# A graph network's dense block: the fused rows are formed in the place of the attention's rows, and the adjacency quarters are asked for one step later

## The chip, the cores and the metric

The kernel runs on one core of a Trainium2 chip. Its time is the device time of one execution in microseconds; the lower the better. The core has five engines[...]: TensorE (PE, matrix products, with its weight loads shown apart as PEld), VectorE (DVE), ScalarE (ACT), GpSimd (POOL) and SyncE (SP, which only issues DMAs). They meet at semaphores. Data lies in SBUF (128 partitions), products land in PSUM, and DMAs move data from and to the chip's main memory.

## The reference

Four graph layers over 4096 nodes of 256 features, with one 4096 x 4096 adjacency of zeros and ones. Each layer normalises its rows, takes the positive part, computes something, and adds it to the rows. The change lies in layer 0, in the part after its attention:

```python
h_enh = silu(_ln(Wh @ fe1_w + fe1_b, fe_ln_g, fe_ln_b)) @ fe2_w + fe2_b
B, C, dt = split(Wh @ W_bcdt + b_bcdt, 3, axis=1)
ab = softmax(dt + A[None, :], axis=1) * B @ abp_w + abp_b
h_part, z = split((Wh * ab) @ W_hz + b_hz, 2, axis=1)
hs = (h_part * silu(z) + h_part * D) @ out_w + out_b
hs = hs * (1.0 + C @ cp_w + cp_b)
comb = concatenate([h_attn, hs], axis=1)
g = sigmoid(silu(_ln(comb @ g1_w + g1_b, g_ln_g, g_ln_b)) @ g2_w + g2_b)
fused = g * h_attn + (1.0 - g) * hs + h_enh
return _ln(fused, ln_g, ln_b)            # and x = x + this
```

`Wh` and `h_attn` come from the attention. Layer 1 divides by the number of ones in each row of the adjacency, so these have to be counted.

## The kernel before

Rows are handled in tiles of 128, four tiles (BT = 4) to a block, eight blocks in all. One large tile `xs` in SBUF holds all 4096 rows. In layer 0 the attention leaves its rows `h_attn` there; at the end of each block's dense part the new rows take their place.

The dense part is the generator `dense(b)`, which yields 30 times. `run_staggered` starts a block every 16 steps and advances all that are active by one step in turn, so that about two blocks are under way: the second half of block b beside the first half of block b + 1. A scheduler then places the instructions of each engine; what the engines run is the order that it makes, not that of the source alone.

In each of a block's first 16 steps `with_counts` also counts a quarter of the adjacency: `ask` has POOL issue a DMA of 128 x 1024 values (L548), and `count` runs two sign activations over it on ScalarE with a running sum (L556). A quarter has one of AHEAD = 4 buffers.

The steps of a block that the prediction speaks of, in order:

- L568: POOL adds `ln_b` to the block's input rows `xt`, which an SP queue has loaded (L565) into the only buffer for them.
- `whT`: TensorE transposes `Wh` in two groups of four (L507); ScalarE copies the first group out of PSUM (L508), VectorE the second (L511). The PSUM pool for transposes has three buffers.
- `bc` (L581), a softmax over part of it (L586 to L596), and `obc` (L598) on POOL.
- `t1` (L607), its normalisation with `fe_off` (L520) on VectorE, and the scaling of it on ScalarE (L523).
- `hidden` turns it and applies silu (L534); `sz` (L631 to L640).
- `henh` (L649): four products and an add of a bias, on VectorE, from PSUM. `hs` (L656): four more. The PSUM pool for products has five buffers.
- `comb` (L663 to L668): `ha`, the block's rows of `xs`, and `hs` are turned in four groups, copied by ScalarE and VectorE in turn. Then POOL takes `dh = ha - hs` (L670) and `hs = hs + henh` (L671).
- `t2` (L677), its normalisation with `gl_off`, `hidden` again, and `f` (L686).
- tanh (L690), L691 and L692 make the fused rows of it; statistics lead to `ol_off`; ScalarE scales (L523); POOL multiplies by `ln_g` (L695) and adds `xt` into `ha` (L696).

In the kernel before, `henh` and `f` carry the same tag in a pool with one buffer per tag, so they take turns in one buffer:

```python
henh = d.tile([P, BT, D], F32, tag="henh", name="henh")   # L645
f = d.tile([P, BT, D], F32, tag="henh", name="f")         # L682
```

Of the kernel before, what the change touches and what calls it, by code (L numbers as in the profile page):

```python
# [11 lines left out]
F32 = mybir.dt.float32  # L12
# [4 lines left out]
ALU = mybir.AluOpType  # L17
# [4 lines left out]
P = 128  # L22
# [6 lines left out]
def run_staggered(gens, period):  # L29

    gens, active, tick = list(gens), [], 0
    while gens or active:
        if gens and tick % period == 0:
            active.append(gens.pop(0))
        for g in list(active):
            if next(g, StopIteration) is StopIteration:
                active.remove(g)
        tick += 1
# [3 lines left out]
def kernel(ctx: ExitStack, tc: tile.TileContext, w: dict, out: bass.AP):  # L42
    nc = tc.nc
    x, adj = w["x"], w["adj"]
    N, D = x.shape
    NT = N // P
    KD = D // P
    BT = 4
# [271 lines left out]
    with ExitStack() as l0:  # L320
# [150 lines left out]
        with ExitStack() as es:  # L471
            d = es.enter_context(tc.tile_pool(name="l0_d", bufs=1))
            AHEAD = 4
# [25 lines left out]
            def wide(t):  # L499

                return t.rearrange("p (o f) -> p o f", o=1).broadcast_to([P, BT, t.shape[1]])
# [26 lines left out]
            def hidden(z, g, b):  # L528

                zT = d.tile([P, KI, BW], F32, tag="zT", name="zT", bufs=2)  # L530
                for k in range(KI):
                    turn(
                        zT[:, k, :], [z[:, i, ts(k, P)] for i in range(BT)],
                        lambda dst, ps: nc.scalar.activation(  # L534
                            dst, ps, AF.Silu, scale=g[:, k : k + 1], bias=b[:, k : k + 1]
                        ),
                    )
                    if k % 2:
                        yield
                return zT  # L540
# [3 lines left out]
            def ask(n):  # L544
                for t, q in asked[len(came) : n]:

                    came.append(code_p.tile([P, QW], BF16, tag="a", name="a", bufs=AHEAD))
                    nc.gpsimd.dma_start(out=came[-1], in_=adj[ts(t, P), ts(q, QW)])  # L548

            def count(g):  # L550

                ask(g + AHEAD)
                t, q = asked[g]
                for v in range(2):
                    sign = code_p.tile([P, QW], BF16, tag="sign", name="sign", bufs=1)
                    nc.scalar.activation(  # L556
                        sign, came[g], AF.Sign, bias=limits[:, v : v + 1],
                        accum_out=over[:, t, v, q : q + 1],
                    )

            def dense(b):
                at = ts(b, BT)
                ha = xs[:, at, :]
                xt = d.tile([P, BT, D], F32, tag="xt", name="xt")
# [80 lines left out]
                henh = d.tile([P, BT, D], F32, tag="henh", name="henh")  # L645
# [33 lines left out]
                yield from normed(t2, "gl")  # L679
                yield  # L680
                g1T = yield from hidden(t2, g_g, g_b)
                f = d.tile([P, BT, D], F32, tag="henh", name="f")  # L682
                for i in range(BT):
                    ps = psm.tile([P, D], F32, tag="mm", name="mm")
                    products(ps, lambda k: g1T[:, k, ts(i, P)], lambda k: g2[:, k, :], KI)
# [7 lines left out]
                yield  # L693
                yield from normed(f, "ol")
                nc.gpsimd.tensor_tensor(f, f, wide(ln_g), ALU.mult)  # L695
                nc.gpsimd.tensor_tensor(ha, f, xt, ALU.add)  # L696

            def with_counts(b):
                at, n = b * BT * NQ, BT * NQ
                for k, _ in enumerate(dense(b)):  # L700
                    if k < n:
                        count(at + k)
                    yield

            ask(AHEAD - 1)
            run_staggered([with_counts(b) for b in range(NB)], 16)


# [360 lines left out]
```

## Time and profile before

| | |
|---|---|
| median of three runs | 3072.19 us (3071.23 to 3072.98) |
| the profiled execution's own time | 3071.94 us |
| its span, first to last instruction | 3070.0 us |
| mean granted TensorE clock over the span | 0.979 |
| PE, PEld, DVE, ACT, POOL busy over the span | 93, 76, 60, 41, 31% |
| dense part of layer 0, from the first quarter counted | 644 to 1256 us |
| of it with counts on ScalarE | 644 to 1126 us |
| one sign over a quarter, and the read of its sum | 1148 ns, 190 ns |
| landing of a quarter's DMA, median | 4.3 us |
| L695 and L696 on POOL | 2348 ns and 2337 ns, medians |

Times count from the span's start. In a line of the timeline the first number is the start, the second the length, then come engine, source line, operation, and written and read tiles; a bracket at the end holds how long the engine had been idle and what ended that. A wait line gives the total, how often, and the longest. An engine that is busy beside others costs nothing unless something waits for it.

### The profile page before, as it was taken

To read this page: it belongs to the slowest core of one execution; us is meant where nothing else is said; L and a number is where in the kernel's file an instruction comes from. 1 tells how busy PE (TensorE), PEld (TensorE's weight loads), DVE (VectorE), ACT (ScalarE), POOL (GpSimd) and SP (SyncE) were. 2 spreads that over 40 slices of the span, in tenths; PEclk is the share of its full clock that TensorE was granted. 3 is DMA by queue.
4 is the path that set the end of the run, shared out by engine and by line. 5 is a ranking of instruction groups with operands and counts; after the bars stand their busy time and mean duration, and the time that the engine had idled before them with its cause. 6 is when DMAs were issued, how large, how long until landed. Compare 5 with 4: busy or idle time off the path is not lost.

```text
span 3070.0 us, 34819 instructions
## 1 busy us (share of the span) xinstructions
PE 2868.8 (93%) x13344; PEld 2341.7 (76%) x13344; DVE 1847.3 (60%) x3298; ACT 1271.1 (41%) x1924; POOL 952.6 (31%) x727
## 2 busy tenths in 40 slices
PE   5799999999999999699968999999999999999999
PEld 4688888866565555588857888788888888888888
DVE  5766766424444444544479888845866666666653
ACT  5555665469999962400044434443211211211211
POOL 3556665534544443100016555561000000000000
PEclk9799999999999999799988999999999999999999
DMA  8566665244544420234222222102111111111100
GB/s 208 130 137 143 127 137 132 66 65 73 79 76 77 75 47 7 88 124 142 91 110 76 89 79 72 71 8 69 59 37 46 49 37 43 52 37 40 53 7 7
DMA packets 105366, 235.18 MB, mean 77 GB/s; under 512 B 10704, under 2 KB 26576, under 8 KB 97008
## 3 DMA queue, kind: packets, MB, share of 16 engines
q0 software_dynamic: 39328, 73.56, 15.6%
q1 hardware_dynamic: 64480, 158.68, 15.0%
q8 instruction: 104, 1.70, 0.2%
q10 hardware_dynamic: 1392, 0.72, 0.1%
q14 instruction: 62, 0.51, 0.1%
HBM read 262.22 MB, written 37.81 MB: 98 GB/s over the span
## 4 chain that ended last, share of the span: by engine, by line
PE 26%; issue 25%; DVE 4%; POOL 2%; DMA 1%; ACT 1%; POOLq 0%; DVEq 0%; ACTq 0%
PE acc L306 11%; PE acc L764 8%; PE s L150 3%; PE mm L150 2%; PE acc L1001 2%; DVE run L229 1%; POOL y L269 1%; DVE y L265 1%; DMA turned<-codesT 1%; POOL out_dram L1014 1%; POOL pl_rs L116 0%; DVE pl_st L121 0%; ACT y L295 0%; ACT h L133 0%; DVE hT L109 0%
## 5 line engine op out<-in xcount | busy, mean ns | idle before, releaser
L306 PE MATMUL acc<-v,y 128*128 128x257 f32 x4096 | 927.7, 385 | 46.1 <-ACT y L295 23.5
L306 PEld LDWEIGHTS acc<-v,y 128*128 128x128 f32 x4096 | 776.3, 192 | 160.5 <-ACT y L295 24.1
L269 POOL TENSOR_TENSOR y<-y,turned 128x1024 f32<-128x1024 f32 x256 | 547.1, 2150 | 313.9 <-DVE y L265 267.1
L295 ACT ACTIVATE y<-y,sdst 128x512 f32<-128x512 f32 x512 | 342.9, 714 | 368.1 <-POOL y L269 367.9
L265 DVE SCALAR_TENSOR_TENSOR y<-ab_row,cdst,b 128x512 f32<-128x512 f32 x512 | 361.7, 742 | 187.9 <-PE acc L306 116.6
L1001 PE MATMUL acc<-v,y 128*128 128x257 f32 x2048 | 454.5, 380 | 0.4 <-DVE rden L1009 0.4
L150 PE MATMUL s<-qT,hT 128*128 128x256 f32 x2048 | 445.2, 380 | 0.7 <-ACT qT L949 0.7
L150 PEld LDWEIGHTS s<-qT,hT 128*128 128x128 f32 x2048 | 389.9, 190 | 53.2 <-ACT qT L949 1.4
L1001 PEld LDWEIGHTS acc<-v,y 128*128 128x128 f32 x2048 | 387.9, 190 | 55.1 <-issue 0.8
L994 ACT ACTIVATE y<-y 128x1024 f32<-128x1024 f32 x128 | 132.2, 1055 | 714.3 <-DVE y L993 710.1
L229 DVE SCALAR_TENSOR_TENSOR run<-turned,sd,run 128x512 f32<-128x512 bf16 x496 | 373.0, 752 | 48.4 <-DMA turned<-codesT 26.8
L1014 POOL DMA_DIRECT2D out_dram<-o x32 | 17.4, 542 | 933.7 <-DVE rden L1009 930.5
L556 ACT ACTIVATE sign<-a,limits 128x1024 bf16<-128x1024 bf16 x256 | 293.9, 1148 | 16.1 <-DMA a<-in_adj_dram 10.4
L764 PE MATMUL acc<-v,eq 128*128 128x512 f32 x1024 | 239.3, 395 | 0.0
L963 DVE SCALAR_TENSOR_TENSOR y<-code,s 128x512 f32<-128x512 bf16 x256 | 175.7, 687 | 100.5 <-PE s L150 100.3
L764 PEld LDWEIGHTS acc<-v,eq 128*128 128x128 f32 x1024 | 192.9, 189 | 44.7 <-DVE eq L760 0.3
L993 DVE TENSOR_TENSOR y<-y,top 128x1024 f32<-128x1024 f32 x128 | 146.2, 1214 | 43.0 <-PE top L987 43.0
L970 DVE TENSOR_TENSOR mx<-mx,y 128x512 f32<-128x512 f32 x224 | 154.9, 691 | 7.4
L362 ACT ACTIVATE turned<-cT,log_wide 128x1024 bf16<-128x1024 bf16 x128 | 141.4, 1105 | 32.1 <-PE cT L357 31.9
L150 PE MATMUL mm<-kept 128*128 128x512 f32 x288 | 135.6, 605 | 9.4 <-ACT kept L508 7.3
L760 DVE TENSOR_SCALAR eq<-code 128x4096 fp32r<-128x4096 bf16 x32 | 73.4, 2292 | 114.9 <-PE acc L764 114.9
L357 PE MATMUL cT<-identb,adj_t 128*128 128x128 bf16 x1024 | 83.2, 226 | 38.1 <-ACT turned L362 19.5
(209 smaller groups left out, 2779.4 us busy)
## 6 DMA issues: line engine op xcount, KB each, us to landing
adj_t<-in_adj_dram POOLq DMA_DIRECT2D x128, 256.0 KB, 4.6
codesT<-turned SPq DMA_DIRECT2D x32, 1024.0 KB, 5.3
a<-in_adj_dram POOLq DMA_DIRECT2D x128, 256.0 KB, 4.2
code<-codesT SPq DMA_DIRECT2D x128, 256.0 KB, 3.8
turned<-codesT SPq DMA_DIRECT2D x32, 1024.0 KB, 4.8
code<-codesT SPq DMA_DIRECT2D x64, 512.0 KB, 4.9
ab_row<-l_ab_d SPq DMA_DIRECT2D x16, 512.0 KB, 4.7
xs<-in_x_dram SPq DMA_DIRECT2D x8, 512.0 KB, 8.3
```

What stands on the lines that cost most here:

```text
L150: nc.tensor.matmul(out=ps, lhsT=lhsT_of(k), rhs=rhs_of(k), start=(k == 0), stop=(k == n - 1))
L229: nc.vector.scalar_tensor_tensor(st["run"], code, self.sd[:, j, 1:2], st["run"], ALU.subtract, ALU.min)
L265: nc.vector.scalar_tensor_tensor(y[:, :, k, :], st["ab"][:, 0, :, :], self.cdst[:, c + k : c + k + 1], st["b"], ALU.add, ALU.max,)
L269: nc.gpsimd.tensor_tensor(y, y, mask[:, :, c % QT : c % QT + 2, :], ALU.subtract)
L295: nc.scalar.activation(y[:, :, k, :], y[:, :, k, :], AF.Exp, bias=self.sdst[:, c + k : c + k + 1],)
L306: nc.tensor.matmul(out=accs[b][r], lhsT=y[:, r, k, :], rhs=self.v[:, c + k, :], start=(c + k == 0), stop=(c + k == NT - 1),)
L556: nc.scalar.activation(sign, came[g], AF.Sign, bias=limits[:, v : v + 1], accum_out=over[:, t, v, q : q + 1],)
L764: nc.tensor.matmul(out=acc, lhsT=eq[:, ts(c, P)], rhs=v1[:, c, :, :], start=(c == 0), stop=(c == NT - 1),)
L963: nc.vector.scalar_tensor_tensor(y[:, :, c : c + 2, :], st["code"][:, :, c : c + 2, :], -BIG / UNIT, ps, ALU.mult, ALU.add,)
L970: nc.vector.tensor_tensor(mx, mx, y[:, :, c : c + 2, :], ALU.max)
L993: nc.vector.tensor_tensor(part, part, top, ALU.subtract)
L1001: nc.tensor.matmul(out=accs[r], lhsT=st["y"][:, r, c, :], rhs=v3[:, c, :], start=(c == 0), stop=(c == NT - 1),)
```

## The change

The fused rows `f` no longer have a buffer of their own turn in the `henh` tag. They are formed in `ha`, the block's rows of `xs`, from the first add (L686) on, and the last step (L696) adds `xt` in place. Apart from that, `count(g)` asks for quarters up to `g + 3` instead of `g + 4`, and two are asked for ahead of the first block instead of three; the buffers for quarters remain four.

```diff
             def count(g):
 
-                ask(g + AHEAD)
+                ask(g + AHEAD - 1)
                 t, q = asked[g]
...
                 g1T = yield from hidden(t2, g_g, g_b)
-                f = d.tile([P, BT, D], F32, tag="henh", name="f")
+
+                f = ha
                 for i in range(BT):
...
                 nc.gpsimd.tensor_tensor(f, f, wide(ln_g), ALU.mult)
-                nc.gpsimd.tensor_tensor(ha, f, xt, ALU.add)
+                nc.gpsimd.tensor_tensor(f, f, xt, ALU.add)
...
-            ask(AHEAD - 1)
+            ask(AHEAD - 2)
             run_staggered([with_counts(b) for b in range(NB)], 16)
```

Lines from L683 on stand one line lower in the changed file; the text keeps the numbers of the kernel before up to the result.

## The prediction

> **What bounds the kernel now.** I read the page first (TensorE 93% busy over the whole span), then the busy time by stretch for the dense part, the only stage that the diff touches. It runs from 644 to 1256 us. Columns of a stretch: length, then PE, PEld, DVE, ACT, POOL busy, TensorE clock, DMA share, GB/s.
>
> ```profile
> 644.00:1126.00 482.00, 449.16 (x1648) 284.23 (x1646) 217.49 (x447) 451.13 (x719) 227.35 (x221) 0.98 0.49 75
> 1126.00:1256.00 130.00, 103.33 (x378) 66.55 (x376) 54.60 (x116) 32.67 (x47) 42.72 (x25) 0.92 0.03 10
> ```
>
> Until 1126 ScalarE counts (two signs of 1.15 us and their 0.19 us reads per quarter) and is full, and TensorE almost so. After 1126 the counts are over and TensorE and its waits alone set the pace. Next the waits of 640 to 1260: the one that the change aims at (us, times, longest).
>
> ```profile
> DVE henh L649 <- POOL xs L696: 44.3, 7, 7.0
> ...
> PE mm L150 <- DVE henh L649: 25.3, 7, 4.2
> ```
>
> VectorE's first `henh` add of a block waits until POOL has finished with the block before's `f`, which has the same buffer; TensorE, with five PSUM buffers, then stands 3.1 to 4.2 us. What ScalarE, the full engine, waited for between 655 and 1126:
>
> ```profile
> ACT f L523 <- DVE ol_off L520: 10.4, 6, 2.1
> ACT sign L556 <- DMA a<-in_adj_dram: 5.7, 6, 1.6
> ACT t L523 <- DVE fe_off L520: 3.2, 5, 0.8
> ACT comb L508 <- PE tp L507: 2.1, 5, 1.0
> ACT whT L508 <- PE tp L507: 1.2, 2, 1.0
> ```
>
> Only 23.5 us with 0.9 of `zT`. So 25 us of TensorE stall can't all come back: ScalarE caps it. The timeline of TensorE and ScalarE in one steady block (start, duration, idle before):
>
> ```profile
> 826.27 1.89 PE L150 MATMUL mm<-kept,sz 128*128 128x256 f32 x8
> 832.32 7.13 PE L150 MATMUL mm<-kept,sz 128*128 128x256 f32 x24 [4.16 <-DVE henh L649]
> 839.29 1.04 PE L507 MATMUL tp<-ident,v 128*128 128x128 f32 x8
> ...
> 842.48 3.64 PE L150 MATMUL mm<-bcw,whT 128*128 128x257 f32 x16
> ```
>
> ```profile
> 839.93 0.59 ACT L508 COPY whT<-tp 128x512 f32<-128x512 f32 x1
> ...
> 863.33 2.93 ACT L523 ACTIVATE t<-t,fe_off,fe_rs 128x512 f32<-128x512 f32 x4 [0.83 <-DVE fe_off L520]
> ```
>
> After the stall TensorE reaches the transposes for `whT` just as ScalarE is ready to copy them: the two are level there. The clock in stretches of 3.41 us (the last three numbers are clock, DMA share, GB/s):
>
> ```profile
> 829.69:833.10 3.41, 0.78 (x4) 0.71 (x5) 1.26 (x4) 3.35 (x6) 3.23 (x3) 1.00 0.05 8
> 833.10:836.51 3.41, 3.41 (x10) 2.70 (x9) 1.03 (x3) 2.58 (x5) 0.00 (x0) 0.50 0.95 228
> 836.51:839.93 3.42, 3.42 (x20) 3.04 (x19) 0.92 (x2) 2.49 (x5) 2.97 (x3) 1.00 0.39 72
> ...
> 1229.06:1232.47 3.41, 2.97 (x13) 2.02 (x12) 0.00 (x0) 2.85 (x5) 0.00 (x0) 0.50 0.00 0
> 1232.47:1235.88 3.41, 3.41 (x10) 2.73 (x9) 0.00 (x0) 1.08 (x2) 0.00 (x0) 0.50 0.00 0
> ```
>
> A nearly empty stretch is followed by one at half clock: the 24 products after the stall took 7.13 us, against 5.45 where the clock stayed (block 5, at 1056.81), 1.7 us lost.
>
> [...] 1229.06 to 1232.47 holds only transposes, and 1232.47 to 1235.88 is still at half clock. [...] L692[...] takes 2.48 us in the middle where POOL runs L598, and 1.23 alone; `henh` and `hs` adds read one operand from PSUM, and stay at 0.41 to 0.48 us beside POOL. [...]
>
> **The change part by part.**
>
> *The asks.* In the source each quarter is asked for one step later. But the scheduler places an ask by when its buffer comes free (four quarters back, in both), and in the two built programs POOL's order, ask by ask, is the same, with the same waits; so are PE's, ACT's and SP's. Cost 0, on both ends: nothing is moved past any queue.
>
> *f in xs.* Nothing is added or removed: adds of 0.42, the activations, and POOL's two products of 2.35 us have the same shapes. The rows of `ha` were last read by L670 and the transposes, earlier on the same path, so no wait is new. Gone is `henh`'s wait for L696. On VectorE the first `henh` add now stands before `ol_off` (L520): 0.42 us inside the 1.16 us that L520 waits for POOL's `ol_rs` anyway (its product ends near 821, the add runs near 823.5), so nothing; if the product were late, ScalarE's L523 would be late by as much.
>
> *The tail* (blocks 6 and 7), where nothing else covers. Block 6: the products for `hs` ended at 1129.88 + 7.13 = 1137.0; without stall and half clock at 1124.49 + 32 x 0.217 = 1131.4. Saved 5.6. Block 7: its stall of 3.12 (clock full). Together 8.7 us. POOL's L568 (to 1135.8), L670 and L671 then end at about 1140.6, before the softmax product on POOL needs it (1148.8 - 5.6).
>
> *Steady blocks 2 to 5.* Let T be the start of ScalarE's `whT` copy. What leads to T is ScalarE's own: the `ol_off` wait (a VectorE chain started by ScalarE's tanh) and the wait for a quarter (asked behind POOL's L696, which hangs on ScalarE's L523) both stay. TensorE now ends `hs` near 828.16 + 5.2 = 833.4, transposes `whT` and two of `comb`, has no free transpose buffer (three), and stands until the copy ends, T + 0.65 (840.6): some 5 us idle. **The stall moves from `henh` to the transposes**, and there the cold restart is no longer covered. 8 transposes remain, 0.87 us warm, 1.75 at half clock, so `bc` begins at T + 1.6 or T + 2.4. From `bc` to `fe_off` are 20.56 us (1065.28 to 1085.84, block 5), and ScalarE gets to L523 at T + 22.3 (862.50 less T, less 0.29 of `comb`). Its wait there: warm 1.6 + 20.56 - 22.3, so none; cold 2.4 + 20.56 - 22.3 = 0.66, plus half of what the products spend at half clock. [...] So 2.1 us (1.4 to 3.0).
>
> Before, `whT`, `comb` and `fe_off` waits together were 1.12, 1.91, 1.25 and 0 in blocks 2 to 5, 4.3 us. After: 4 x 2.1 = 8.4. Block 1 has its `whT` earlier; it loses its 1.28 of `comb` wait and may get about 0.9 back at `fe_off`: -0.4. Steady sum: +3.7 (all warm: -5.6; all at the worst phase: +8).
>
> *Sum.* -8.7 + 3.7 = -5.0. The profiled execution is 3071.94 (span 3070.0 and 1.9 around it): 3066.9. The median of the runs is 0.25 above it: **3067.2 us**.
>
> **The rivals.**
>
> 1. *Warm restart.* The gap counts less than I think, and ScalarE loses its PE-made waits as well: -8.7 - 4.3 - 1.3 = -14.3, 3057.9 us. For it: block 5 kept its clock through 3.53 us, and had no `fe_off` wait. Against: a 5 us gap with transposes at both ends. [...]
>
> 2. *Slower.* Place: the `bc` and first `t` products after the copy. If the half clock lasts two windows longer than I take it (as after 1229, where it held for two), each block pays 3.4 more: +17 over five, net +12, 3084. It is slower than before from 1.0 us a block (2 us more at half clock), and by 0.2% from 2.2 us a block.
>
> 3. *The tail does not give.* The last blocks wait for something else that is just as late; nothing in the tail's timeline is (ScalarE waits 11.8 us for the very transposes), so only -1 to +4: 3071 to 3076.
>
> 4. *Late asks.* If the asks really came one step later, the one quarter per block that is late today (behind L696) would be later by a count, two signs or 2.5 us: seven blocks, 18 us, 3085. The order on POOL speaks against it.
>
> **How the numbers follow.** 0.2%, 6.1 us, is about what a measurement tells from no change: 3066.0 to 3078.3. Forecast (moved stall, cold) 0.55, of which 0.17 ends beyond 6.1 us (its own range is 3063 to 3072); rival 1 with its middle 0.27, all but 0.01 faster; rival 2 0.07; rival 3 0.09; rival 4 0.02. Faster 0.43, within 0.48, slower 0.09. The range leaves out rivals 2 and 4 and the fastest end: 3057 to 3075.
>
> **What would show it.** DVE's `henh` no longer waits for L696, and PE's wait for `henh` falls from 25.3 to under 2 us. PE instead waits at the transposes (L507) for ACT's `whT` copy, about 5 us in each of four blocks, and the stretch after it shows a clock of 0.5. ACT's `fe_off` wait before the end of the counts rises from 3.2 to about 9 us, `comb` and `whT` fall to nearly 0, `ol_off` (10.4) and the quarters (5.7) stay. From the last sign to the first row of the next stage takes 122 instead of 130 us. I am wrong if `fe_off` falls (rival 1), if the transposes keep TensorE at full clock, or if the quarters' wait grows.

## The result, and the profile after

The changed kernel takes 3061.44 us (median of 6 runs, 3058.41 to 3063.83), the kernel before 3072.09 us (median of 6, 3070.02 to 3072.98): ratio 0.9962, 95% interval 0.9950 to 0.9974. That is 10.65 us less, where 5.0 were forecast. The profiled execution of the changed kernel is the fastest of the six (3058.41 us, span 3056.5), so the profiles differ by more than the medians; the place of each difference has to be read first. From here on, lines from L683 on are one higher in the changed kernel (tanh is L691, the product with `ln_g` L696, the addition of `xt` L697); experiments made from the kernel before keep its numbers.

Three marks divide the span: the start of the first sign, the start of the last sign, and the first transposes of layer 1 (L144), with which the next stage's TensorE work begins.

| us | before | after | difference |
|---|---|---|---|
| start to first sign | 643.8 | 639.1 | -4.7 |
| first sign to last sign | 480.6 | 481.1 | +0.5 |
| last sign to first transposes of layer 1 | 136.5 | 125.5 | -11.1 |
| from there to the end | 1809.1 | 1810.9 | +1.8 |

The first row lies ahead of everything that the diff touches; over the kernels profiled below it runs from 636.6 to 643.8 us. The last row lies behind it. The two rows between make -10.6 us, and so agree with the medians. So the gain is the third row, and **the stretch in which ScalarE counts has gained nothing, though five of the seven stalls lay in it**.

The busy times of the dense part after, in the columns of the prediction (the second stretch ends at the first statistics of layer 1, where it took 130 us before):

```profile
639.10:1121.40 482.30, 451.20 (x1647) 285.10 (x1647) 220.99 (x449) 450.51 (x719) 227.38 (x221) 0.97 0.49 76
1121.40:1241.00 119.60, 99.61 (x380) 64.42 (x378) 57.69 (x113) 32.69 (x48) 43.22 (x25) 0.93 0.03 10
```

The waits of 640 to 1260 us after:

```profile
PE tp L507 <- ACT whT L508: 15.3, 4, 4.7
...
DVE henh L649 <- PE mm L150: 12.5, 14, 1.3
```

The waits for L696 on VectorE (44.3 us) and for `henh` on TensorE (25.3 us) have gone; VectorE now waits for TensorE's products. TensorE has a new one instead: four times it stands at the transposes for ScalarE's copy of `whT`. And ScalarE, from 650 to 1121.5 us:

```profile
ACT xs L523 <- DVE ol_off L520: 10.4, 6, 2.1
ACT sign L556 <- DMA a<-in_adj_dram: 6.7, 8, 1.6
ACT t L523 <- DVE fe_off L520: 5.4, 5, 1.7
ACT zT L534 <- PE tp L507: 2.0, 3, 1.4
```

`ol_off` is the same to the tenth, `comb` and `whT` are gone, `fe_off` has grown from 3.2 to 5.4. The timeline of TensorE in the steady block that the prediction showed:

```profile
822.20 7.07 PE L150 MATMUL mm<-kept,sz 128*128 128x256 f32 x32
829.11 1.04 PE L507 MATMUL tp<-ident,v 128*128 128x128 f32 x8
829.98 0.60 PE L507 MATMUL tp<-ident,xs 128*128 128x128 f32 x4
830.93 0.66 PE L507 MATMUL tp<-ident,xs 128*128 128x128 f32 x4 [0.35 <-DVE whT L511]
836.27 1.97 PE L507 MATMUL tp<-ident,hs 128*128 128x128 f32 x8 [4.68 <-ACT whT L508]
```

All 32 products for `henh` and `hs` now run through (7.07 us, at 0.22 each). The idle time of 4.16 us from ahead of the last 24 of them stands 4.68 us long before the last transposes, and these take 1.97 us instead of 1.04. The clock in the same stretches of 3.41 us:

```profile
829.69:833.10 3.41, 1.55 (x13) 1.07 (x10) 1.49 (x3) 1.94 (x4) 0.24 (x1) 1.00 1.06 245
833.10:836.51 3.41, 0.24 (x1) 0.25 (x2) 0.00 (x0) 3.25 (x6) 3.39 (x4) 0.96 0.22 35
836.51:839.93 3.42, 3.42 (x14) 3.06 (x14) 0.72 (x2) 3.39 (x7) 3.40 (x3) 0.54 1.03 153
```

An almost empty stretch, then one at 0.54: the half clock has moved from the `hs` products, which nobody waited for before the copy, to `bc`, which everything waits for. After the last sign there is neither stall nor half clock at those places:

```profile
1120.24 7.07 PE L150 MATMUL mm<-kept,sz 128*128 128x256 f32 x32
...
1188.30 7.07 PE L150 MATMUL mm<-kept,sz 128*128 128x256 f32 x32
...
1219.02 7.15 PE L150 MATMUL mm<-kept,zT 128*128 128x256 f32 x32
1245.65 2.17 PE L144 MATMUL tp<-ident,h 128*128 128x128 f32 x8 [19.48 <-ACT h L133]
```

### The profile page after: what moved, and what is told of

It reads as the page before. It is cut to its first block, busy times and chain, and to the rows that moved or that the text cites. A ratio compares the mean times of both kernels' runs of the same rounds, so it can differ in the third digit from the quotient of the medians.

```text
span 3056.5 us, 34808 instructions
## 1 busy us (share of the span) xinstructions
PE 2866.7 (94%) x13344; PEld 2336.3 (76%) x13344; DVE 1853.8 (61%) x3298; ACT 1270.6 (42%) x1924; POOL 952.8 (31%) x727
## 4 chain that ended last, share of the span: by engine, by line
PE 28%; issue 25%; DVE 3%; POOL 2%; ACT 1%; DMA 0%; POOLq 0%; DVEq 0%; ACTq 0%
PE acc L306 13%; PE acc L765 8%; PE s L150 3%; PE acc L1002 2%; PE mm L150 2%; POOL y L269 1%; DVE run L229 1%; POOL pl_rs L116 1%; POOL out_dram L1015 1%; DVE y L265 0%; DVE pl_st L121 0%; DMA turned<-codesT 0%; ACT h L133 0%; DVE hT L109 0%; ACT y L295 0%
## 5 line engine op out<-in xcount | busy, mean ns | idle before, releaser
L556 ACT ACTIVATE sign<-a,limits 128x1024 bf16<-128x1024 bf16 x256 | 293.9, 1148 | 16.7 <-DMA a<-in_adj_dram 11.1
```

The lines of the kernel that those rows point to most:

```text
L556: nc.scalar.activation(sign, came[g], AF.Sign, bias=limits[:, v : v + 1], accum_out=over[:, t, v, q : q + 1],)
```

## The experiments

### Where the gain is: the blocks apart, and the asks apart

`f` can be formed in `ha` in some blocks and in the shared buffer in the others. A block's `f` delays the next block's `henh`; so the blocks from 5 on govern the two stalls after the last sign, and blocks 0 to 4 the five before it.

```diff
-                f = d.tile([P, BT, D], F32, tag="henh", name="f")
+                f = ha if b >= 5 else d.tile([P, BT, D], F32, tag="henh", name="f")   # the end alone
+                f = ha if b < 5 else d.tile([P, BT, D], F32, tag="henh", name="f")    # the steady part alone
```

The end alone:

> Only the last three blocks (5, 6 and 7) form f in ha; the blocks 0 to 4 keep the shared buffer, and the quarters are asked for as in the kernel before. So only the stalls of blocks 6 and 7, which come after the last sign, go. Theory A (while ScalarE counts, it sets the pace, and a stall of TensorE taken away there comes back elsewhere; the gain is made after the last sign alone): all of the changed kernel's gain, -11 us, 3061; from the last sign's end to the first transposes of the next stage 124 to 126 us instead of 135.4; the waits of ScalarE before the last sign as in the kernel before. Rival B (each of the seven stalls gives its share of the gain): two sevenths of 10.65, -3 us, 3069.

The steady part alone:

> The other half: blocks 0 to 4 form f in ha, the blocks 5 to 7 keep the shared buffer; quarters asked for as before. The stalls of blocks 1 to 5 go, those of blocks 6 and 7 stay. Theory A: no gain, 3072 to 3076 (+0.5 as the changed kernel's profile has it between the first and the last sign, +3.7 as forecast); TensorE waits for ScalarE's whT copy in four blocks, 15 us in all. Rival B: five sevenths of the gain, -8 us, 3064.

The asks alone (`ask(g + AHEAD - 1)` and `ask(AHEAD - 2)`, `f` as before):

> Only the asks of the change (up to g + 3, two ahead of the first block); f keeps its turn in the shared buffer. Theory A: nothing, 3072 within 2 us, since the order on every engine is that of the kernel before. Rival C (a part of the gain comes from the asks): 2 us or more away from the kernel before, to the changed kernel's side.

Measured on one chip, against a median of 3072.41 us for the kernel before:

| | median us | ratio, 95% interval | first to last sign | last sign to layer 1 |
|---|---|---|---|---|
| the end alone | 3059.72 | 0.9962 (0.9949 to 0.9976) | 481.4 | 125.5 |
| the steady part alone | 3074.66 | 1.0010 (1.0003 to 1.0016) | 484.5 | 139.1 |
| the asks alone | 3071.15 | 0.9997 (0.9989 to 1.0006) | 481.5 | 136.5 |

The end alone gives the whole gain (-12.7 us), the steady part alone costs 2.3 us, and their sum, -10.4, comes near the change's -10.65. The asks do nothing that can be told, as the equal order on the engines had it. With the shared buffer in the blocks that matter there, three executions took 480.6, 481.4 and 481.5 us from the first sign to the last, so differences under 1 us in that column say nothing. The waits of TensorE, first in the run of the end alone and then in that of the steady part alone:

```profile
PE mm L150 <- DVE henh L649: 18.7, 5, 4.2
```

```profile
PE tp L507 <- ACT whT L508: 15.9, 4, 4.7
...
PE mm L150 <- DVE henh L649: 6.6, 2, 3.5
```

Five stalls of 18.7 us in all (those that the end alone keeps) are traded for four waits of 15.9 us. In this execution all four blocks behind such a wait ran `bc` in 4.71 to 5.32 us, where 3.64 is full clock, and the stretch with the signs grew by 3.9 us; in the changed kernel's profile one block of four escaped (4.44, 5.32, 4.79 and 3.64), and it grew by 0.5. The forecast for that stretch, +3.7, lies inside what the same edit does from one execution to the next.

### What holds ScalarE's copy: the amount of its work, or what it waits for?

My reason was that ScalarE is full. To take work off it, every sign was cut to half of its quarter's columns, in both kernels; half of the ones are then not counted.

```diff
-                        sign, came[g], AF.Sign, bias=limits[:, v : v + 1],
+                        sign[:, 0:512], came[g][:, 0:512], AF.Sign, bias=limits[:, v : v + 1],
```

With the kernel before:

> The kernel before, whose signs and sums take half of a quarter's columns only (so half of the ones are not counted); all DMAs stay. [...] Theory A: TensorE with its stalls sets the pace, so the stretch from the first to the last sign takes the time of TensorE's work and stalls, 455 to 475 us instead of 482; 3045 to 3065 in all. To be set against the changed kernel with the same halves.

With the changed kernel:

> The changed kernel with the same halves of the signs and sums (half of the ones are not counted). Theory A: with ScalarE out of the way each of the five stalls before the last sign is worth what it takes from TensorE, 3.1 to 4.2 us and up to 1.7 of half clock, so that this one is 11 + 5 x 3.5 to 5 x 5.5 = 28 to 38 us faster than the kernel before with halves. Rival B' (the stalls before the last sign are worth nothing whoever sets the pace, because the block's chain through f, ol_off and the next block is as long): 11 us faster.

A sign of half a quarter took 0.72 us (median), where a whole one takes 1.15. Both became slower than the kernel before, not faster: 3099.86 us (1.0081, 1.0063 to 1.0099) and 3084.42 us (1.0036, 1.0023 to 1.0050). So the forecast of 3045 to 3065 us for the first missed. The scheduler plans shorter signs ahead, so that they end after 350 us and nothing is left to count beside the later blocks; the total can't be set against that of whole signs. But the two can be set against each other. In the medians they are 15.4 us apart, where Theory A had 28 to 38 and Rival B' 11. The `henh` stalls of the shared buffer, with halves, are these:

```profile
765.30 8.34 PE L150 MATMUL mm<-kept,sz 128*128 128x256 f32 x24 [3.83 <-DVE henh L649]
847.17 8.37 PE L150 MATMUL mm<-kept,sz 128*128 128x256 f32 x24 [3.91 <-DVE henh L649]
929.88 7.98 PE L150 MATMUL mm<-kept,sz 128*128 128x256 f32 x24 [4.33 <-DVE henh L649]
1010.81 8.46 PE L150 MATMUL mm<-kept,sz 128*128 128x256 f32 x24 [3.06 <-DVE henh L649]
```

Three lie before the last sign (990.2), and four after it (3.06, 3.11, 3.12, 3.12). With `f` in `ha` all seven are gone. From first to last sign that is worth 350.3 - 349.3 = 1.0 us; from there to layer 1 it is worth 297.5 - 278.2 = 19.3 us, or 4.8 a stall, which is 12.4 us of idle time, 4.7 of half clock (the 24 products took 3.0 and 1.6 us over 5.45 in two blocks) and 2.2 more, half of which lies in the last products (8.76 against 7.66 us). So a stall counts after the last sign and not before, though here ScalarE was busy for only 297 of 350 us: the cover does not need a full engine. But the halved signs brought a limit of their own. From 655 to 990 us ScalarE now waited for quarters, in the shared buffer's run for 29.8 us and in the other for 28.6, where whole signs had 5.7 and 6.7:

```profile
ACT sign L556 <- DMA a<-in_adj_dram: 28.6, 24, 3.4
```

So this pair shows a cover that halved signs have, and for whole signs it only points to a place to look. The way from the quarter to TensorE shows in the timeline of ScalarE, POOL and TensorE, in the changed kernel with halves:

```profile
762.25 2.37 POOL L697 TENSOR_TENSOR xs<-xs,xt 128x1024 f32<-128x1024 f32 x1
...
764.56 1.63 POOL L548 DMA_DIRECT2D a<-in_adj_dram  x3
...
770.68 0.72 ACT L556 ACTIVATE sign<-a,limits 128x512 bf16<-128x512 bf16 x1 [3.41 <-DMA a<-in_adj_dram]
...
773.94 0.56 ACT L508 COPY whT<-tp 128x512 f32<-128x512 f32 x1
...
774.56 1.12 PE L507 MATMUL tp<-ident,xs 128*128 128x128 f32 x4 [6.86 <-ACT whT L508]
```

POOL ends L697, issues the asks that stood in line behind it, the quarter lands, ScalarE can go on with its signs, and only after them copies `whT`, for which TensorE has stood 6.86 us. In the changed kernel itself, with whole signs, the same chain is there and the wait in it shorter:

```profile
825.41 2.36 POOL L697 TENSOR_TENSOR xs<-xs,xt 128x1024 f32<-128x1024 f32 x1
```

```profile
820.82 2.08 ACT L523 ACTIVATE xs<-xs,ol_off,ol_rs 128x256 f32<-128x256 f32 x4 [2.08 <-DVE ol_off L520]
...
833.23 1.15 ACT L556 ACTIVATE sign<-a,limits 128x1024 bf16<-128x1024 bf16 x1 [1.56 <-DMA a<-in_adj_dram]
...
835.65 0.56 ACT L508 COPY whT<-tp 128x512 f32<-128x512 f32 x1
```

L697 ends at 825.41 + 2.36 = 827.77, and the sign that had waited 1.56 us for its quarter starts at 833.23. **The same instruction on POOL therefore holds up the block by two ways**: through the buffer of `henh` and TensorE, and through the quarter and ScalarE. Before the change TensorE and ScalarE reached the copy together (transposes from 839.29, copy at 839.93). The change removed the first way. But the late quarter is only 1.56 of the 4.68 us for which TensorE stands in this block; the rest of the second way is ScalarE's own: from L523 at 820.82 to the copy it has nine signs to do. After the last sign the second way doesn't exist.

### Both ways shortened: the last two steps on VectorE

If so, an earlier end of L697 shortens both ways. (The second alone, with the asks placed ahead of the arithmetic on POOL, was not run.) A step of this shape (128x1024, f32) takes POOL 2.35 us (L696 in the changed kernel, at 822.98) and took VectorE 1.23 in the run below (L696 at 825.09). The order of TensorE, ScalarE and SP is not changed by the move.

```diff
-                nc.gpsimd.tensor_tensor(f, f, wide(ln_g), ALU.mult)
-                nc.gpsimd.tensor_tensor(f, f, xt, ALU.add)
+                nc.vector.tensor_tensor(f, f, wide(ln_g), ALU.mult)
+                nc.vector.tensor_tensor(f, f, xt, ALU.add)
```

In the changed kernel:

> The changed kernel, whose last two steps of a block (times ln_g, L696, and plus xt, L697) run on VectorE instead of POOL; the orders of TensorE, ScalarE and SP stay as they are. Theory G (before the last sign two ways lead from the end of L697 to the copies of whT: the one that the change took away, and the quarter that POOL asks for behind L697, which lands some 5.5 us later and holds up ScalarE's signs and so the copy): the ask comes some 5 us earlier, ScalarE's wait for quarters falls from 6.7 to under 2 us, TensorE's wait for the whT copy from 15.3 to about 10; 1.2 us for each of five blocks, and 2.2 us at the end of the last block, 8 in all: 3053. Rival A' (ScalarE's own work and the ol_off chain set the copy, and the late quarter only takes up slack): only the 2 us at the end, 3059. Rival H (1.23 us twice a block in line on VectorE delays henh and TensorE): 3061 or more.

In the kernel before:

> The kernel before with the same two steps on VectorE. L696 then ends some 2.3 us earlier, so that the stall at henh falls from 3.1 to 4.2 us to 1 to 2, in the tail too, and the late quarter is asked for earlier. Theory G: about 5 us in the tail (two stalls, with less half clock), 2 at the end of the last block, up to 5 before the last sign: 3060 to 3065; forming f in ha on top of it is worth 5 to 10 us instead of 11. Rival A' (without the quarters): 7 us, 3065. Rival H: 3070 or more.

And with `f` in `ha` for blocks 5 to 7 only:

> The last two steps of a block on VectorE in all blocks, and f in ha for the blocks 5 to 7 only; blocks 0 to 4 keep the shared buffer. Theory J (before the last sign the short stall at henh is worth having: it parts TensorE's idle time into two pieces of under 2 us, so that the clock is kept, where f in ha makes one piece of 2.5 to 3.2 us with a restart at half clock; after the last sign f in ha saves what is left of two stalls): the stretch with the signs as in the run with the shared buffer, 472 us, the time after it 1.5 to 2.5 us shorter, 3048 to 3050. Rival K (f in ha is worse on VectorE everywhere, because the two steps then stand among the henh adds): 3053 to 3056.

| two steps on VectorE | median us | ratio, 95% interval | first to last sign | last sign to layer 1 |
|---|---|---|---|---|
| `f` in `ha` in all blocks | 3055.50 | 0.9947 (0.9934 to 0.9959) | 475.9 | 125.1 |
| shared buffer in all blocks | 3050.97 | 0.9926 (0.9912 to 0.9939) | 470.9 | 126.6 |
| `f` in `ha` in blocks 5 to 7 | 3049.66 | 0.9925 (0.9911 to 0.9938) | 473.8 | 124.2 |

Each ratio is to the kernel before on the same chip (3072.49 us for the first two rows, 3071.08 for the third).

The stretch with the signs, which the change had left at 481.1 us, falls to 475.9: in it ScalarE no longer waits for a late quarter (after 655 us that wait is gone from the list) and TensorE's wait for `whT` falls from 15.3 to 11.4:

```profile
PE tp L507 <- ACT whT L508: 11.4, 4, 3.2
```

Theory G asked for 3053 and under 2 us of waiting for quarters, and the theory without the quarters for 3059; the run lies between at 3055.5. Both have a part in it. The quarters account for the gain, 5.2 us of stretch for 6.7 us of waiting. What is left of TensorE's wait is ScalarE's own work, as Rival A' has it: in the same block ScalarE now runs from L523 through its nine signs to the copy without a stop, and that takes 836.28 - 822.98 = 13.3 us, where it took 14.8 with the late quarter:

```profile
822.98 2.08 ACT L523 ACTIVATE xs<-xs,ol_off,ol_rs 128x256 f32<-128x256 f32 x4 [2.08 <-DVE ol_off L520]
...
836.28 0.57 ACT L508 COPY whT<-tp 128x512 f32<-128x512 f32 x1
```

What I had not expected is the second row: **with the two steps on VectorE the shared buffer is no worse than `f` in `ha`, and in the medians 4.5 us better**. The two intervals overlap by 0.0005, but the slowest of its five runs (3054.50) is faster than the fastest of the other five (3055.02). It also beat every forecast for it, of which the best was 3060. The timeline of TensorE tells why. With `f` in `ha`:

```profile
824.35 7.07 PE L150 MATMUL mm<-kept,sz 128*128 128x256 f32 x32
...
836.90 1.97 PE L507 MATMUL tp<-ident,hs 128*128 128x128 f32 x8 [3.17 <-ACT whT L508]
```

With the shared buffer:

```profile
821.23 5.45 PE L150 MATMUL mm<-kept,sz 128*128 128x256 f32 x24 [1.90 <-DVE henh L649]
...
829.98 1.14 PE L507 MATMUL tp<-ident,hs 128*128 128x128 f32 x8 [0.99 <-ACT whT L508]
830.96 3.64 PE L150 MATMUL mm<-bcw,whT 128*128 128x257 f32 x16
```

The idle time is about the same, 3.2 against 2.9 us, but in one piece it is followed by half clock (8 transposes in 1.97, `bc` in 5.34 us), and in two pieces it is not (1.14 and 3.64). Over blocks 2 and 3 the single piece costs 1.97 us each time for the transposes, and 5.34 and 4.12 for `bc`; the two pieces 1.14 and 3.64 in each. In sum that is 3.94 against 2.28 us and 9.46 against 7.28, 3.8 us more in these two blocks, and the whole stretch differs by 5.0. That the clock makes the difference is read from these lines; no run changed the clock alone. Its size is that of two executions, and they are unlike: the profiled one of the shared buffer was the second fastest of its five, and the other the slowest. A stall upstream, where the path has room, kept TensorE from running into a longer one where it has none.

The third row keeps the stall before the last sign and takes it away after it. Its time is that of theory J (3048 to 3050), and the part after the last sign is 2.4 us shorter than with the shared buffer. The stretch before it came out at 473.8 instead of 472, with a restart at half clock in block 2 that the profile of the shared buffer does not have: after a stall of 1.91 us the 24 products took 7.13 us (at 827.85), where they took 5.45 there after 1.90. It has the lowest median here, but can't be told from the kernel with the shared buffer.

### The copies dealt otherwise

The wait that was new is one for ScalarE's copy. VectorE can take it, with ScalarE given another one so that it keeps three copies a block:

```diff
-                        onto if k else nc.scalar.copy,           # whT
+                        onto,
...
-                        onto if k % 2 else nc.scalar.copy,       # comb
+                        onto if k == 1 else nc.scalar.copy,
```

> The changed kernel, with the copies of the transposes dealt otherwise: VectorE takes both whT copies, ScalarE three of the four comb copies instead of two, so that ScalarE has as many copies as before (three a block), but TensorE's next products, bc, no longer hang on a ScalarE copy. Theory D (the stall that moved to the transposes, with its restart at half clock, costs ScalarE its 5.4 us of waits for fe_off before the last sign, and nothing more): TensorE's wait for whT 15.3 -> under 2, fe_off 5.4 -> under 1, time 5 us below the changed kernel, 3056. Rival E (ScalarE loses as much at another wait, such as comb or the quarters, as soon as this one is gone): no difference to the changed kernel, 3061.

3059.76 us, 0.9961 (0.9949 to 0.9974): not to be told from the changed kernel, as rival E has it. In its profile the stretch with the signs took 478.0 us, some 3 less than in that of the changed kernel. As the edit also changed the order in which ScalarE runs its signs, and there is one profile of each, whether that is a gain stays open. `fe_off` did fall from 5.4 to 1.8 us and TensorE's wait for `whT` vanished, as theory D has it; but TensorE then stood for ScalarE's copies of `comb`:

```profile
PE tp L507 <- ACT comb L508: 17.1, 5, 4.4
```

and the quarters' wait rose from 6.7 to 9.1 us. So it seems that the copy of `whT` was only the place where the wait surfaced. Then all six copies went to VectorE, in both kernels (`onto` at both places).

In the changed kernel:

> The changed kernel, with all six copies of the transposes (whT and comb) of a block on VectorE; ScalarE loses three of 0.58 us a block. Theory A (ScalarE sets the pace until the last sign): 1.75 us a block over seven blocks, 12 us, and with the copies TensorE's wait at the transposes and most of ScalarE's 5.4 us for fe_off: 12 to 17 us below the changed kernel, 3044 to 3049. Rival F (with three copies of 0.69 us more in line on VectorE, the bound passes to TensorE or to a VectorE chain, ol_off among them): a gain under 5 us, 3056 to 3061, and ScalarE's waits grow by what it was relieved of.

In the kernel before:

> The kernel before with the same six copies on VectorE: the stall at henh is there, and ScalarE has 12 us less to do. Theory A: TensorE (449 us busy and 25 of stall in 482) now sets the pace together with ScalarE, so that the relief brings less than it does in the changed kernel: 0 to 8 us below the kernel before, 3064 to 3072; so forming f in ha is worth more here than 11 us, 15 to 20. Rival B (a stall gives its own share whatever ScalarE does): the relief brings the same in both, and f in ha is worth 11 us here too.

None of the four forecasts came: 3077.63 us (1.0018, 1.0012 to 1.0025) and 3081.61 us (1.0029, 1.0019 to 1.0038), both slower than the kernel before. Taking 12 us of copies off ScalarE made the dense part longer in the changed kernel, by 6.3 us up to the last sign and 12.0 after it. In the kernel before it became 3.6 us shorter up to the last sign and 12.9 longer after it. The scheduler places the work differently here: behind the last sign TensorE has 43 and 44 more instructions and is busy for 12.1 and 12.9 us longer, so what the part after it grew by is for the most part work that has moved there. Up to the last sign ScalarE's waits grew, those for quarters alone from 6.7 to 16.6 us in the changed kernel and from 5.7 to 14.6 in the kernel before, as Rival F had it for the changed kernel. And here too `f` in `ha` is the worse one up to the last sign, 487.4 us against 477.0; the mean granted clock over the whole span was 0.973 against 0.976. In the changed kernel with the six copies on VectorE, TensorE waits for ScalarE's scaled rows:

```profile
PE tp L507 <- ACT t L523: 27.3, 21, 4.1
```

Without the edit that wait was 6.8 us in 5 instances. Whether the copies in VectorE's line or the new order does the harm is not settled by these two runs.

## Why the prediction was right or wrong

**The forecast** of 3067.2 us is 5.8 us above the result, which lies inside the range of 3057 to 3075. The gain, 10.65 us, is twice the 5.0 that were forecast. The single likeliest class was no difference above 0.2%; the kernel is 0.38% faster.

**The asks**: right. Alone they give 0.9997.

**`f` in `xs`**: right that nothing waits for the new place of the rows. `ol_off` stayed at 10.4 us.

**The tail**: the mechanism was right and the term too small, -8.7 against -11.1 us in the profile. The run that has it alone shows -11.0 there in its profile, and -12.7 in the median of the whole kernel. Block 6 gave 5.5 for 5.6 forecast: from the last sign's start to the transposes that follow its `hs` products 12.45 us became 6.95. Block 7 gave 3.4 for 3.12 forecast (from those transposes to the ones after its own `hs` products 71.44 us became 68.06). The remaining 2.2 us were not in the sum; 1.6 of them lie in the last products, which took 7.15 us instead of 8.74. Ahead of them half clock held for two stretches of 3.41 us before (from 1229.06, in the prediction's lines) and for one in the changed kernel:

```profile
1215.12:1218.53 3.41, 2.97 (x13) 1.95 (x13) 0.00 (x0) 2.84 (x5) 0.00 (x0) 0.50 0.00 0
1218.53:1221.94 3.41, 3.41 (x18) 2.92 (x19) 0.42 (x1) 1.95 (x3) 0.00 (x0) 1.00 0.00 0
```

With the two steps on VectorE and `f` in `ha`, where the stalls are gone as well, the products took 8.78; so this piece does not go with the stalls, and isn't the change's. To have 1.6 us of it was luck.

**The steady blocks**: that the stall moves to the transposes, that it is followed by half clock and that ScalarE then waits longer for `fe_off`, was right (4.68, 2.90, 4.72 and 3.03 us; 1.97 us for transposes, `bc` up to 5.32). The size, +3.7, was +0.5 in one profile and +3.9 in the other. The step that failed is "4 x 2.1": it took block 2, with its gap of 5 us, for all four, and the time at half clock in the 2.1 was only an estimate of mine. Blocks 3 and 5 had a shorter stall before (3.52 and 3.53 against 4.16) and have a shorter gap after, and block 5 kept its clock. `fe_off` came to 5.4 us instead of 8.4. Three other waits of ScalarE, which the sum left as they were, grew in return: for quarters from 5.7 to 6.7 us, for `zT` from 0.9 to 2.0, for `bc` from nothing to 0.3. The first of these the prediction had named as a sign of being wrong ("if the quarters' wait grows"); the growth is small, but the sign came. The worst case of +8 is +7.3 by its own terms (4 x 3.0 - 4.3 - 0.4).

**"ScalarE caps it"**: right as a bound, and short as a reason. Nine kernels here have whole signs and three copies a block on ScalarE. In every one of them ScalarE is busy for 449.2 to 450.2 us from the first sign to the last, so that stretch can differ by ScalarE's idle time only: 30.5 us before, 31.8 after, 31.3 with the end alone, 35.2 with the steady part alone, and 26.5, 21.5 and 24.4 in the three kernels with two steps on VectorE. A stall of TensorE is worth there what it makes ScalarE wait, and no more. The stalls of the kernel before made it wait for little, the 3.3 us of `comb` and `whT`, and what came in their place, at `fe_off` and `zT`, made it wait as long. What the prediction missed lies in its own words that `ol_off` and "the wait for a quarter" "both stay". They did, but the second hangs on the very instruction whose hold on `henh` the change removes: with L696 and L697 made shorter that wait went, and the stretch gave up 5 to 10 us at once.

**Rival 1** (3057.9, a warm restart) is 3.5 us from the result, nearer than the forecast, yet not by its mechanism: three of four restarts in the changed kernel ran at half clock. **Rival 2** (slower from half clock) is what the steady part does when it is alone, but at 2.3 us, where the rival had 12; the tail outweighs it. **Rivals 3 and 4** fell with the runs of the end alone and the asks alone.

**The gaps and the clock.** In the changed kernel a gap of 2.90 us (to 909.90) was followed by half clock (`bc` in 5.32 us) and one of 3.03 (to 1059.86) was not (3.64). With two steps on VectorE and `f` in `ha` in all blocks one of 2.52 (to 911.05) was (transposes in 1.97), and with `f` in `ha` in blocks 5 to 7 one of 1.91 was (24 products in 7.13, at 827.85) and another of 1.91 was not (5.45, at 972.92). So no single length of a gap is the limit in this kernel. What told the gaps apart better is how full TensorE was in a stretch of 3.41 us; the last section has it. As for the transposes, the prediction has one place where a stretch of transposes alone (2.97 us busy, from 1229.06) was followed by half clock. The lines from 1215.12 above are a place with the other outcome: again 2.97 us of transposes alone at half clock, and full clock after them. These two don't settle what transposes alone do to the clock.

## What to carry to other kernels

Before counting a removed wait as gained, follow the event that ended it to everything else that it releases: if a second way leads from there to the same later instruction and is as long, only the difference between the two is gained. Here the way through a DMA queue, an ask standing in line behind arithmetic on POOL, was together with ScalarE's signs as long as the way through a buffer. Making the common event earlier gave 21 us where removing one of its ways gave 11; in the profiles the difference lies before the last sign, 9.7 us against none. It also helps to find the engine whose work in a stretch is the same in every variant: only its waits can be gained. A stall that lies off the path may also be worth leaving where it is, if what follows would otherwise idle in one longer piece and restart at half clock on the path, as here with 3.17 us in one piece against 1.90 and 0.99 in two.

## What the runs showed of the hardware

With two steps on VectorE, the same idle time of about 3 us in block 2 cost TensorE no half clock when it came in two pieces (1.90 and 0.99 us; transposes in 1.14 and `bc` in 3.64) and 2.5 us when it came in one (3.17 us; 1.97 and 5.34). An empty stretch isn't needed. In the kernel with `f` in `ha` for blocks 5 to 7 the clock fell at 829.15 us, after a stretch in which TensorE was busy for 1.50 us:

```profile
825.74:829.15 3.41, 1.50 (x7) 1.17 (x7) 3.27 (x7) 3.31 (x7) 1.01 (x2) 1.00 0.43 54
829.15:832.57 3.42, 3.42 (x10) 2.71 (x9) 0.51 (x2) 3.32 (x7) 0.43 (x2) 0.50 1.01 244
```

In the traces of the kernel before and of the changed kernel all changes of the granted clock between 640 and 1300 us (16 and 14) lie whole multiples of 3.413 us apart. Both traces were cut on that grid, up to 1260 us, and the 334 stretches at full clock sorted by TensorE's busy time. Of the 14 with under 1.4 us all were followed by half clock, and of the 307 with 2.1 us or more none. Of the 13 between, one was, with 1.43 us (from 907.92 in the changed kernel). An estimate from these numbers fits the two pieces: with a gap of 1.90 us and work on both sides a stretch of 3.41 us holds at least 1.51 us of work, while a gap of 3.17 us can leave it nearly empty. A gap of 1.91 us was followed by half clock once and once not (827.85 and 972.92, in the run of the lines above), so gaps of that length are at the edge here. These are counts for the f32 products and transposes of this stage; no run varied a gap for its own sake.

A quarter asked for behind POOL's arithmetic was ready 5.5 us after the ask's start at 827.71 in the changed kernel (its sign at 833.23), and 6.1 us after it where three asks were issued in one go (764.56 to 770.68, in the changed kernel with halves), against a median landing of 4.2 us (127 asks of the kernel before from 640 to 1260 us; 124 of the changed one, the same; the table ahead has 4.3).
